# A graph layer's node stage: the second tile's relu(x - mean) on ScalarE, one step behind VectorE's moments

## The chip, the cores and the metric

The kernel runs on one core of a Trainium2 chip. The time is the device time of one execution in microseconds, as a median over several runs, and a profile is one execution with every instruction recorded. Engines are named as the profile names them: PE (TensorE, with PEld for its weight loads), DVE (VectorE), ACT (ScalarE), POOL (GpSimd) and SP (SyncE). A "q" behind a name marks what the engine's sequencer does, such as issuing a DMA.

## The reference

There are 12,500 nodes with 160 features and 400,000 edges sorted by target node. The features are normalized, passed through a relu, and sent over the edges with weights that a small network makes for each edge:

```
h = max((x - mean) / sqrt(var + 1e-5), 0)            # per node
y0, y1 = (h[:, :64] @ W_l1_0) * a, (h[:, 64:] @ W_l1_1) * a    # a: one number per node
s0, s1 = the same with W_sc0, W_sc1
w = silu(e4_len @ fc_W1 / 4) @ fc_W2 / 8             # per edge, 192 numbers
mid = products of w, y[src] and the edge's attributes # per edge
z = sum of mid over the edges of each target node
out = x + sin(pi/8) * s + cos(pi/8) * (z @ W_l2) * a
```

Because the reciprocal deviation is positive, max((x - mean) * r, 0) equals r * max(x - mean, 0). The kernel therefore computes relu(x - mean) first and applies r and a together, later, as one number per node.

## The kernel before

A tile is 128 nodes or 128 edges. There are 98 node tiles and 3125 edge tiles. The program has three parts.

**The node stage (L269 to L411)** makes y and s for all nodes. It loads x into `acc`, which stays in SBUF until the end as the sum to be written out. Its unit is a step q of two tiles (HN = 2), and four steps make a group of eight tiles (GN = 8). Ninety-eight node tiles come first, then 40 tiles of gathered rows (`xr`, fetched by gather_x() on POOL), whose y is needed by some edge blocks in edge order; that is 138 tiles in 69 steps. A step passes through these functions:

- center() on DVE: for each of the two tiles bn_stats (L326), bn_aggr (L327, mean and variance into `mv`) and h = max(x - mean, 0) (L328). In a group's last step ACT takes the square root of the variances (L332).
- scales() on DVE: in a group's last step the reciprocal (L340) and the product with a (L341), giving `ra`.
- turn_rows() on PE: four transposes into PSUM (L347, L348). out_of_psum() on ACT: their copy to SBUF as `hT` (L354).
- map_rows() on PE: the products with the weights, four matmuls a tile (L363, L364).
- leave() on ACT: the results times `ra` out of PSUM as `ys` (L375), two instructions; in a group's last step also the DMA that stores y to DRAM, issued from ACT's queue (L378 for nodes, L380 for gathered rows).
- add_s() on DVE: in a group's last step s is added to `acc` (L386), for node tiles only.

The loop at L404 writes the order out by hand: in iteration q it calls each function for step q minus a lag (scales 1, leave 4, out_of_psum 2, turn_rows 1, map_rows 3, center 0, add_s 5), in this sequence. Inside `manual_schedule` PE, ACT and DVE keep the written order; each works through its own queue and waits only where a semaphore holds it. POOL and SP are ordered by a planner, which also merges the second hand-ordered block into the first where it thinks its operands are there: so the edge weights' scaling on DVE (L234 and on) stands between two instructions of center(). In iteration 16 first_nodes() reads the edges' targets on DVE.

**relate() (L140)** follows on DVE once the node stage's last scales() is done. It turns targets into positions inside windows. The buffers that it uses are given to the main stage afterwards.

**The main stage (from L438)** goes over the edges in blocks of four tiles (GT = 4). POOL gathers y rows by an indirect DMA for each tile (L475) into `yg`, which has twelve buffers of four tiles; SP loads the edge attributes (L466, L515); PE makes the edge weights (L506), ACT scales them (L423), DVE multiplies (L429 to L436), PE sums by target (L557), and the sums of each window go through two more products into `acc` (L604).

Buffers come from pools: `nd` holds three buffers each of h and hT, `ns` three each of the small tiles (`st`, `mv`, `ra`), `nd_pt` two PSUM buffers for the transposes and `nd_po` six for the maps' results, that is three steps.

Of the kernel before, what the change touches and what calls it, by code (L numbers as in the profile page):

```python
# [10 lines left out]
F32 = mybir.dt.float32  # L11
I32 = mybir.dt.int32
AF = mybir.ActivationFunctionType
ALU = mybir.AluOpType
# [4 lines left out]
P = 128  # L19
M0 = 64  # L20
M1 = 32
D = M0 + 3 * M1
# [13 lines left out]
HN = 2  # L36
# [9 lines left out]
def kernel(  # L46
# [19 lines left out]
    nc = tc.nc  # L66
# [62 lines left out]
    def first_nodes():  # L129

        nc.vector.tensor_copy(drel, dst_i)
        nc.vector.memset(neg, -float(ZR))
        if full:
            nc.vector.tensor_reduce(neg[:, :full], drel[:, :full * WT].rearrange("p (s t) -> p s t", t=WT),
                                    AX.X, ALU.min, negate=True)
        if full < NWIN:
            nc.vector.tensor_reduce(neg[:, full:NWIN], drel[:, full * WT:T], AX.X, ALU.min, negate=True)
        nc.gpsimd.partition_all_reduce(negb, neg, P, bass_isa.ReduceOp.max)
# [61 lines left out]
    def node_weights():  # L200
        nc.vector.memset(wn0, 0.0)
        nc.vector.memset(wnr, 0.0)
        nc.scalar.dma_start(wn0[0:M0, 0, :], w_l1_0)
        nc.scalar.dma_start(wn0[0:M0, 1, :], w_sc0)
        for c in range(3):
            s = slice(M1 * c, M1 * (c + 1))
            nc.scalar.dma_start(wnr[LO + c::3, 0, s], w_l1_1)
            nc.scalar.dma_start(wnr[LO + c::3, 1, s], w_sc1)
        nc.vector.tensor_scalar(wn0[:, 0, :], wn0[:, 0, :], 1.0 / math.sqrt(M0), None, ALU.mult)
        nc.vector.tensor_scalar(wn0[:, 1, :], wn0[:, 1, :], C_S / math.sqrt(M0), None, ALU.mult)  # L210
        nc.vector.tensor_scalar(wn1[:, 0, :], wnr[:, 0, :], 1.0 / math.sqrt(M1), None, ALU.mult)
        nc.vector.tensor_scalar(wn1[:, 1, :].rearrange("p (u c) -> p c u", c=3),
                                wnr[:, 1, :].rearrange("p (c u) -> p c u", c=3), C_S / math.sqrt(M1), None, ALU.mult)

    def edge_weight_loads():
        nc.gpsimd.memset(w1, 0.0)
        for i in range(P // FC_IN):
            nc.sync.dma_start(w1[FC_IN * i:FC_IN * (i + 1), FC_H * (i % 2):FC_H * (i % 2 + 1)], fc_w1)
        for i in range(2):
            for to, of, m in ((0, 0, M0), (M0, 2 * M0, M1), (M0 + M1, M0, M0), (2 * M0 + M1, 2 * M0 + M1, M1)):  # L220
                nc.sync.dma_start(w2[FC_H * i:FC_H * (i + 1), to:to + m], fc_w2[:, of:of + m])
        nc.gpsimd.memset(wor, 0.0)

        def o1(c):
            return slice(M0 + M1 * c, M0 + M1 * (c + 1))

        nc.sync.dma_start(wor[0:M0 + M1, 0, 0:M0], w_l2_0)
        for rows, k, c in ((slice(96, P), 0, 0), (slice(0, 32), 1, 1), (slice(32, 64), 1, 2)):
            nc.sync.dma_start(wor[rows, k, o1(c)], w_l2_1[M0:, :])
        for rows, k, c in ((slice(64, P), 1, 0), (slice(0, 64), 2, 1), (slice(64, P), 2, 2)):  # L230
            nc.sync.dma_start(wor[rows, k, o1(c)], w_l2_1[0:M0, :])
# [37 lines left out]
    with (  # L269
        tc.tile_pool(name="nr", bufs=1) as nrp,  # L270
        tc.tile_pool(name="ny", bufs=2) as ny,
        tc.tile_pool(name="ns", bufs=3) as ns,
        tc.tile_pool(name="nd", bufs=3) as nd,
        tc.tile_pool(name="nd_pt", bufs=2, space=PSUM) as nd_pt,
        tc.tile_pool(name="nd_po", bufs=6, space=PSUM) as nd_po,
    ):
        yss, mvs, ras, hs, pts, hTs, poss = ({} for _ in range(7))
        loads = groups + [(NT + t, min(GN, RT - t)) for t in range(0, RT, GN)]
        steps = [(g, n, j, min(HN, n - j)) for g, n in loads for j in range(0, n, HN)]
        if RT:  # L280
# [3 lines left out]
        def load_x(g, n):  # L284
            if g + n == NT and N % P:
                nc.gpsimd.memset(acc[:, NT - 1, :], 0.0)
            node_dma(g, n, lambda rows, t, p: nc.sync.dma_start(acc[:p, g + t.start:g + t.stop, :],
                                                                by_tile(x[rows, :])))

        def gather_x():  # L290

            hi = nrp.tile([P, nr, GT], I32, name="hi")
            ai = nrp.tile([P, nr, GT], I32, name="ai")
            hf = nrp.tile([P, nr, GT], F32, name="hf")
            nf = nrp.tile([P, nr, GT], F32, name="nf")
            of = src_sb[:, RS * GT:RS * GT * (nr + 1)].rearrange("p (r c) -> p r c", c=RS * GT)[:, :, 0:GT]
            nc.vector.tensor_scalar(hi, of, 7, None, ALU.arith_shift_right)
            nc.vector.tensor_copy(hf, hi)
            nc.vector.tensor_copy(nf, of)
            nc.vector.tensor_scalar(hf, hf, -float(P * NT - 1), None, ALU.mult)  # L300
            nc.vector.scalar_tensor_tensor(nf, nf, float(NT), hf, op0=ALU.mult, op1=ALU.add)
            nc.vector.tensor_copy(ai, nf)
            table = attr.rearrange("p i -> (p i)").unsqueeze(1)
            for t in range(RT):
                c = (t // GT + 1) * RS * GT + t % GT
                nc.gpsimd.indirect_dma_start(
                    out=xr[:, t, :], out_offset=None, in_=x,
                    in_offset=bass.IndirectOffsetOnAxis(ap=src_sb[:, c:c + 1], axis=0))
                nc.gpsimd.indirect_dma_start(
                    out=ar[:, t:t + 1], out_offset=None, in_=table,  # L310
                    in_offset=bass.IndirectOffsetOnAxis(ap=ai[:, t // GT, t % GT:t % GT + 1], axis=0))

        def rows_of(g, n):
            return acc[:, g:g + n, :] if g < NT else xr[:, g - NT:g - NT + n, :]

        def center(q):

            g, n, j, m = steps[q]
            xt = rows_of(g, n)
            if j == 0:  # L320
                mvs[g] = ns.tile([P, GN, 2], F32, name="mv")
            mv = mvs[g]
            h = nd.tile([P, HN, D], F32, name="h")
            for k in range(m):
                st = ns.tile([P, 6], F32, name="st")
                nc.vector.bn_stats(st, xt[:, j + k, :])  # L326
                nc.vector.bn_aggr(mv[:, j + k, :], st)  # L327
                nc.vector.tensor_scalar(h[:, k, :], xt[:, j + k, :], mv[:, j + k, 0:1], 0.0, ALU.subtract, ALU.max)  # L328
            hs[q] = h
            if j + m == n:  # L330
                ra = ns.tile([P, GN], F32, name="ra")
                nc.scalar.activation(ra[:, :n], mv[:, :n, 1], AF.Sqrt, bias=eps)  # L332
                ras[g] = ra

        def scales(q):

            g, n, j, m = steps[q]
            if j + m == n:
                ra = ras[g]
                nc.vector.reciprocal(ra[:, :n], ra[:, :n])  # L340
                nc.vector.tensor_mul(ra[:, :n], ra[:, :n], a_sb[:, g:g + n] if g < NT else ar[:, g - NT:g - NT + n])  # L341
# [47 lines left out]
        with tc.manual_schedule(engines=engines):  # L389
            load_x(0, HN)  # L390
            nc.sync.dma_start(a_sb, attr)
            node_weights()
            load_x(HN, min(GN, NT) - HN) if NT > HN else None
            nc.sync.dma_start(src_sb, src)
            for k, (g, n) in enumerate(groups[1:]):
                load_x(g, n)
                if k == 4:
                    nc.sync.dma_start(dst_i, dst)
            if len(groups) <= 5:
                nc.sync.dma_start(dst_i, dst)  # L400
            edge_weight_loads()
            last = len(steps) - 1
            mid = len(steps) - -(-RT // HN)
            for q in range(len(steps) + 5):  # L404
                if q == min(4, last) and RT:
                    gather_x()
                if q == min(16, mid):
                    first_nodes()
                for stage, lag in ((scales, 1), (leave, 4), (out_of_psum, 2), (turn_rows, 1), (map_rows, 3), (center, 0),
                                   (add_s, 5)):  # L410
                    if 0 <= q - lag <= last:  # L411
                        stage(q - lag)
    with tc.tile_pool(name="rel", bufs=1) as rp, tc.tile_pool(name="rel_p", bufs=1, space=PSUM) as rpp:
# [24 lines left out]
    with (  # L438
# [178 lines left out]
        with order:  # L617
# [10 lines left out]
            for b in range(NB):  # L628
                g, k = divmod(b, K)
                if b + AHEAD < NB:  # L630
                    load(b + AHEAD)
                q, r = divmod(b, EG * K)
# [27 lines left out]
    with (  # L660
# [10 lines left out]
        n = nc.values_load(far_i[0:1, 0:1], min_val=0, max_val=1)  # L671
        with tc.For_i(0, n, 1) as _:
            with tc.For_i(0, ZR, P) as r:
                nc.sync.dma_start(z_d[ds(r, P), :], zero)
            with tc.For_i(0, TP // GT, 1) as g:
# [32 lines left out]
                for k in range(GT):  # L708
# [4 lines left out]
                    m = fp.tile([P, ZC], F32, name="f_m")  # L713
# [80 lines left out]
```

## Time and profile before

| | us |
|---|---|
| median of 3 runs (lowest, highest) | 4042.76 (4033.68, 4043.74) |
| the profiled execution's own time | 4041.36 |
| its span, first to last instruction | 4039.5 |
| busy in the span: PE, DVE, ACT, POOL | 3237.9, 2921.0, 2690.3, 3021.9 |
| node stage on DVE, first bn_stats to last scales() | 11.6 to 168.8 |
| relate() on DVE | 168.9 to 193.1 |
| first instruction of ACT in the main stage | 204.2 |

A row of the profile's groups reads: line, engine, operation, out<-in, shapes and count, then busy time, mean ns of one, and the idle time of the engine just before, with what ended it. A row of the timeline reads: start, duration, engine, line, operation, and in brackets the idle time before it with what released it. Two instructions in a row on one engine can overlap by some 0.1 us. The profile's times are counted from the span's start.

### The profile page before, as it was taken

The numbers are of one execution on the slowest core, as the hardware profiler recorded it, in microseconds if no ns is written. First come the engines' busy times: TensorE is split into PE (matmuls) and PEld (weight loads), VectorE is DVE, ScalarE is ACT, GpSimd is POOL, SyncE is SP. The second block draws the span as 40 slices with busy tenths as digits, with TensorE's granted clock in tenths as the row PEclk, the third lists the DMA queues.
The fourth block names the chain that finished last, engine by engine and source line by source line (L and its number), as shares of the span: only waits on it lengthen the run. The fifth ranks groups of instructions, "written<-read, shape, count | busy, mean of one in ns | idle before, by whom it ended". The sixth has DMA issues, their size and how long they took to land.

```text
span 4039.5 us, 62548 instructions
## 1 busy us (share of the span) xinstructions
PE 3237.9 (80%) x17505; PEld 2352.5 (58%) x17505; DVE 2921.0 (72%) x7558; ACT 2690.3 (67%) x9543; POOL 3021.9 (75%) x3177
## 2 busy tenths in 40 slices
PE   6689888878787887887777877887787777778887
PEld 5567666555555555555555555555555555555555
DVE  7889777777776776777776777777777767777776
ACT  5488677766666666666666666666666666666665
POOL 7667777777777777777777777777777777777776
PEclk9899999999999899999999999999999999999898
DMA  6333333222232223232223232323233222343232
GB/s 194 107 82 89 80 80 82 74 74 76 74 76 74 74 73 76 74 76 74 74 73 77 74 76 74 76 71 77 74 76 77 74 74 74 76 123 76 71 83 77
DMA packets 244949, 326.49 MB, mean 81 GB/s; under 512 B 67290, under 2 KB 194342, under 8 KB 244342
## 3 DMA queue, kind: packets, MB, share of 16 engines
q0 software_dynamic: 151280, 256.22, 25.6%
q1 hardware_dynamic: 74322, 54.52, 4.7%
q10 hardware_dynamic: 18996, 11.72, 0.9%
q8 instruction: 141, 2.31, 0.2%
q14 instruction: 210, 1.72, 0.1%
HBM read 302.92 MB, written 19.28 MB: 80 GB/s over the span
## 4 chain that ended last, share of the span: by engine, by line
DVE 23%; POOL 22%; issue 20%; DMA 20%; PE 7%; ACT 2%; DVEq 1%; ACTq 0%; POOLq 0%
POOL yg L475 22%; DMA yg<-y_d,src_sb 20%; DVE tmp L431 5%; DVE tmp L429 4%; PE pz L557 3%; DVE pr L434 3%; DVE pr L433 2%; DVE acc L604 2%; DVE sel L539 2%; DVE pr L436 2%; PE pw L506 2%; DVE pr L432 1%; DVE sel L537 1%; PE px L484 1%; ACT pw L423 1%
## 5 line engine op out<-in xcount | busy, mean ns | idle before, releaser
L475 POOL DMA_INDIRECT yg<-y_d,src_sb x3085 | 2929.8, 950 | 958.0 <-issue 749.9
L557 PE MATMUL pz<-pr,sel 128*128 128x256 f32 x6250 | 1628.1, 407 | 0.6 <-DVE pr L436 0.6
L423 ACT ACTIVATE pw<-pw,ev 128x96 f32<-128x96 f32 x3125 | 985.3, 315 | 839.9 <-PE pw L506 750.7
L557 PEld LDWEIGHTS pz<-pr,sel 128*128 128x128 f32 x6250 | 1239.5, 208 | 159.3 <-issue 0.9
L506 PE MATMUL pw<-w,hT 64*128 64x192 f32 x6250 | 761.3, 364 | 649.9 <-DVE pr L436 639.6
L506 PEld LDWEIGHTS pw<-w,hT 64*128 64x128 f32 x6250 | 516.5, 195 | 1043.1 <-DVE pr L436 874.0
L429 DVE TENSOR_TENSOR tmp<-yg,pw 128x384 f32<-128x384 f32 x782 | 432.2, 553 | 952.2 <-DMA yg<-y_d,src_sb 951.5
L564 ACT ACTIVATE zs<-pz 32x64 f32<-32x64 f32 x3126 | 669.8, 214 | 41.7
L431 DVE TENSOR_REDUCE tmp<-tmp 128x128 f32<-128x384 f32 x782 | 463.6, 593 | 27.0
L539 DVE TENSOR_TENSOR sel<-sel,pw 128x384 f32<-128x384 f32 x782 | 432.7, 553 | 26.9
L562 ACT ACTIVATE zs<-pz 32x192 f32<-32x192 f32 x1042 | 337.8, 324 | 155.4 <-PE pz L557 134.3
L434 DVE TENSOR_TENSOR pr<-pw,yg 128x384 f32<-128x384 f32 x782 | 427.0, 546 | 0.0
L484 PE MATMUL px<-xe,w 32*128 32x512 f32 x782 | 293.5, 656 | 73.2 <-issue 65.5
L489 ACT ACTIVATE hT<-px 128x512 f32<-128x512 f32 x391 | 217.7, 595 | 169.3 <-PE px L484 162.5
L432 DVE TENSOR_TENSOR pr<-pw,yg 128x256 f32<-128x256 f32 x782 | 323.4, 414 | 0.0
L433 DVE TENSOR_TENSOR pr<-pw,yg 128x256 f32<-128x256 f32 x782 | 322.6, 413 | 0.0
L537 DVE TENSOR_TENSOR sel<-iota,pw 128x128 f32<-128x128 f32 x782 | 216.5, 277 | 58.4 <-ACT pw L424 57.3
L581 PE MATMUL px<-wc,za 128*128 128x96 f32 (+1 forms) x1566 | 256.4, 304 | 0.4 <-ACT za L574 0.4
L581 PEld LDWEIGHTS px<-wc,za 128*128 128x128 f32 x1566 | 211.2, 205 | 62.7 <-issue 45.5
L595 PE MATMUL px<-os,place 128*128 128x160 f32 x1044 | 221.2, 336 | 0.5 <-ACT os L584 0.5
L436 DVE TENSOR_TENSOR pr<-pw,tmp 128x128 f32<-128x128 f32 x782 | 217.9, 279 | 0.0
L604 DVE SCALAR_TENSOR_TENSOR acc<-px,a_sb,acc 128x160 f32 x522 | 197.6, 379 | 12.6 <-PE px L595 3.3
(97 smaller groups left out, 1747.5 us busy)
## 6 DMA issues: line engine op xcount, KB each, us to landing
yg<-y_d,src_sb POOLq DMA_INDIRECT x3085
xe<-in_e SPq DMA_DIRECT2D x784, 32.0 KB
y_d<-ys ACTq DMA_DIRECT2D x12, 640.0 KB
acc<-in_x SPq DMA_DIRECT2D x11, 640.0 KB
out<-acc SPq DMA_DIRECT2D x11, 640.0 KB
raw<-in_e SPq DMA_DIRECT2D x32, 192.0 KB
yr_d<-ys ACTq DMA_DIRECT2D x5, 640.0 KB
yg<-yr_d SPq DMA_DIRECT2D x10, 320.0 KB
```

Of the source, the lines that this page charges most:

```text
L423: nc.scalar.activation(pw[:, k, 0:96], pw[:, k, 0:96], AF.Copy, scale=ev[:, k, 0:1])
L429: nc.vector.tensor_tensor(tmp[:, :n, 0:3, :], y1, wt[:, :n, NW:NW + 3].unsqueeze(3).to_broadcast([P, n, 3, M1]), ALU.mult)
L431: nc.vector.tensor_reduce(tmp[:, :n, 3, :], tmp[:, :n, 0:3, :].rearrange("p t c u -> p t u c"), AX.X, ALU.add)
L432: nc.vector.tensor_mul(pr[:, :n, 192:PC], wt[:, :n, 96:160], yg[:, :n, 0:M0])
L433: nc.vector.tensor_mul(pr[:, :n, 0:M0], wt[:, :n, 0:M0], yg[:, :n, 0:M0])
L434: nc.vector.tensor_mul(pr[:, :n, 96:192].rearrange("p t (c u) -> p t c u", c=3), wt[:, :n, M0:96].unsqueeze(2).to_broadcast([P, n, 3, M1]) ...
L475: nc.gpsimd.indirect_dma_start(out=yg[:, k, :], out_offset=None, in_=y_d, in_offset=bass.IndirectOffsetOnAxis(ap=src_sb[:, t:t + 1], axis=0))
L506: nc.tensor.matmul(pw[:, k, 0:NW], hT[r, o:o + P], w2[r, :], start=True, stop=True)
L539: nc.vector.tensor_tensor(sel[:, :, 0:3, :], sel[:, :, 3:4, :].to_broadcast([P, n, 3, WN]), wt[:, :n, NW:NW + 3].unsqueeze(3).to_broadcast ...
L557: nc.tensor.matmul(pz[:, 0:PC], sels[g][:, t % TG, :, :], pr[:, k, :], start=t % WT == 0, stop=last)
L564: nc.scalar.activation(zs[:, 192 + M0 * c:192 + M0 * (c + 1)], pz[WN * c:WN * (c + 1), 192:PC], AF.Copy)
L581: nc.tensor.matmul(po[:m, lo:hi], za[:, k, :m], wc[:, k, lo:hi], start=k == 0, stop=k == 1)
```

## The change

The second tile of each step no longer gets its h on DVE. DVE writes the negated mean into a new 128x1 tile `less` instead, and a new function, center_second(), computes relu(x + less) on ACT in the next iteration. Since h is now complete one step later, turn_rows, out_of_psum, map_rows, leave and add_s each move one step back, and the loop runs one iteration longer. The tile h moves to a pool of its own with four buffers. First tiles stay as they were.

```diff
+        tc.tile_pool(name="nh", bufs=4) as nh,
...
-            h = nd.tile([P, HN, D], F32, name="h")
+            h = nh.tile([P, HN, D], F32, name="h")
             for k in range(m):
                 st = ns.tile([P, 6], F32, name="st")
                 nc.vector.bn_stats(st, xt[:, j + k, :])
                 nc.vector.bn_aggr(mv[:, j + k, :], st)
-                nc.vector.tensor_scalar(h[:, k, :], xt[:, j + k, :], mv[:, j + k, 0:1], 0.0, ALU.subtract, ALU.max)
+                if k == 0:
+                    nc.vector.tensor_scalar(h[:, k, :], xt[:, j + k, :], mv[:, j + k, 0:1], 0.0, ALU.subtract, ALU.max)
+                else:
+                    less = ns.tile([P, 1], F32, name="less")
+                    nc.vector.tensor_scalar(less, mv[:, j + k, 0:1], -1.0, None, ALU.mult)
+                    lesses[q] = less
...
+        def center_second(q):
+
+            g, n, j, m = steps[q]
+            if m > 1:
+                nc.scalar.activation(hs[q][:, 1, :], rows_of(g, n)[:, j + 1, :], AF.Relu, bias=lesses.pop(q))
...
-            for q in range(len(steps) + 5):
+            for q in range(len(steps) + 6):
...
-                for stage, lag in ((scales, 1), (leave, 4), (out_of_psum, 2), (turn_rows, 1), (map_rows, 3), (center, 0),
-                                   (add_s, 5)):
+                for stage, lag in ((scales, 1), (center_second, 1), (leave, 5), (out_of_psum, 3), (turn_rows, 2), (map_rows, 4),
+                                   (center, 0), (add_s, 6)):
```

More of the change, by code (lines that the diff above doesn't have):

```diff
@@ L276 @@
     ):
-        yss, mvs, ras, hs, pts, hTs, poss = ({} for _ in range(7))
+        yss, mvs, ras, hs, lesses, pts, hTs, poss = ({} for _ in range(8))
         loads = groups + [(NT + t, min(GN, RT - t)) for t in range(0, RT, GN)]
```

## The prediction

> **What bounds the kernel now.** I read the list of costly groups first, then GpSimd's timeline, then walked back from it.
>
> ```profile
> L475 POOL DMA_INDIRECT yg<-y_d,src_sb x3085 | 2929.8, 950 | 958.0 <-issue 749.9
> ```
> ```profile
> 204.28 0.94 POOL L475 DMA_INDIRECT yg<-y_d,src_sb  x1 [0.30 <-issue]
> 216.88 0.95 POOL L475 DMA_INDIRECT yg<-y_d,src_sb  x1 [11.65 <-DVE pr L436]
> ...
> 4017.51 0.95 POOL L475 DMA_INDIRECT yg<-y_d,src_sb  x1 [0.30 <-issue]
> ```
>
> Of GpSimd's 958.0 us of idle time before L475, 6.56 lie before the first gather (138.49 us), 11.65 at 216.88, and the rest is a regular 0.30 per gather. 48 gathers fill the twelve yg buffers; then GpSimd waits until block 1's products free one, and from 216.88 it issues without a pause until the last, at 4018.76: 3801.9 us. The tail behind it is 4039.5 - 4018.8 = 20.7. Nothing in the change touches these two terms, 94.6% of the span. What can move is the restart at 216.88.
>
> The waits name what the restart hangs on:
>
> ```profile
> SPq L466 <- DVE far_i L183: 70.8, 1, 70.8
> ACT ev L522 <- DMA raw<-in_e: 31.5, 1, 31.5
> ```
>
> SyncE can't issue the main stage's first loads (193.21) before VectorE ends relate() (193.1); ScalarE starts at 204.22 when the last of them lands; products of blocks 0 and 1 take until 216.8. relate() starts at 168.87, right after VectorE's last scales(). So a microsecond that VectorE gains or loses in the node stage (11.6 to 168.9 us) moves the end by a microsecond. In that stage:
>
> ```profile
> 71.76:80.39 8.63, 7.13 (x49) 5.84 (x49) 7.72 (x27) 6.13 (x13) 6.80 (x7) 1.00 0.36 105
> 146.34:154.12 7.78, 7.55 (x54) 7.39 (x54) 6.41 (x27) 5.33 (x13) 5.95 (x7) 0.77 0.56 151
> 161.26:168.36 7.10, 6.31 (x48) 5.23 (x48) 6.20 (x26) 5.18 (x13) 5.44 (x6) 1.00 0.59 167
> ```
>
> Each row is one group of eight tiles, four steps (busy time of PE, weight load, DVE, ACT, POOL, then granted clock). DVE carries most (7.72 of 8.63) except in the two gathered groups at a granted clock of 0.62 and 0.77, which PE fills. A group's last step on both engines:
>
> ```profile
> 78.64 0.31 DVE L326 BATCH_NORM_STATS2 st<-acc 128x6 f32<-128x160 f32 x1
> 78.98 0.18 DVE L327 BATCH_NORM_AGGREGATE mv<-st 128x2 f32<-128x6 f32 x1
> 79.27 0.30 DVE L328 TENSOR_SCALAR h<-acc,mv 128x160 f32<-128x160 f32 x1
> 79.49 0.32 DVE L326 BATCH_NORM_STATS2 st<-acc 128x6 f32<-128x160 f32 x1
> 79.84 0.18 DVE L327 BATCH_NORM_AGGREGATE mv<-st 128x2 f32<-128x6 f32 x1
> 80.06 0.30 DVE L328 TENSOR_SCALAR h<-acc,mv 128x160 f32<-128x160 f32 x1
> 80.39 0.20 DVE L340 RECIPROCAL ra<-ra 128x8 f32<-128x8 f32 x1
> ```
> ```profile
> 78.06 1.08 ACT L375 ACTIVATE ys<-po,ra 128x320 f32<-128x320 f32 x2 [1.50 <-PE po L364]
> 79.16 0.37 ACTq L378 DMA_DIRECT2D y_d<-ys  x1
> 79.57 0.60 ACT L354 ACTIVATE hT<-pt 128x512 f32<-128x512 f32 x1 [0.44 <-ACT ys L375]
> 80.07 0.29 ACT L332 ACTIVATE ra<-mv,eps 128x8 f32<-128x8 f32 x1
> ```
>
> A DVE step has no gaps: 1.66 us, or 1.75 where an h takes 0.40. ACT reaches the square root (80.07) just as the moments are there, and DVE's reciprocal follows it at once. ACT has 1.5 us spare, in front of ys.
>
> **VectorE's removed work.** 69 second tiles lose h (L328). It took 0.30, and the next instruction began 0.22 after it did (76.67 to 76.89); in the steps of 1.75 another 0.09. In its place comes a 128x1 multiply:
>
> ```profile
> 4026.18 0.15 DVE L668 TENSOR_SCALAR spare<-lane 128x1 f32<-128x1 f32 x1
> ```
>
> 0.15 long, overlapping the next bn_stats by 0.08 as L341 does (72.00 to 72.08), so 0.07. First tiles' h starts 0.07 later after its aggregate than second tiles' (0.29 against 0.22), with an extra wait; the multiply may need that too, to reuse `less`. So an ordinary step falls from 1.65 to 1.50 or 1.57; I take 1.54, and the 0.40 form gone with h.
>
> **ScalarE's added work.** 69 Relus of 128x160 with a bias pointer. Nearest row: L375's 128x160 form, 0.39 long, two beginning 0.28 apart (169.90 to 170.45 for both); I take 0.29. The Trainium skill ("ScalarE: Activation LUTs", What ACT_TABLE_LOAD costs) gives 280 ns + 0.833 per element with a pointer bias, overlapped by 93: an estimate of 0.32 apart, 0.03 more per group on the path below. The bounds are 0.28 and 0.41 (no overlap). The same page's rules for kernel authors say that relu belongs on VectorE, not ScalarE. By that rule each moved tile costs 0.29 where it saved 0.11: a loss of 69 x 0.18 = 12 us if ACT paced the stage. The rows say it doesn't: 6.13 + 4 x 0.29 = 7.3 of 8.63. But the rule bites at one place.
>
> **The wait that it adds.** The Relu is first in ACT's queue in each iteration and can't start before VectorE's `less` of the step before. Queued behind it are two ys, hT and, in a group's last step, the square root, for which DVE's scales() wait. Counted from the start of DVE's last step: `less` visible 0.12 + Relu 0.29 + ys 0.82 (73.56 to 74.38) + hT 0.49 + square root 0.29 + release 0.03 = 2.04. DVE has its own 1.54, and so waits 0.5, where it waited 0.1 and its step was 1.75.
>
> **A group, summed.** Ordinary: scales 0.32 + 3 x 1.54 + add_s 1.40 + 2.04 = 8.38, against 8.63: -0.25. Gathered (no add_s, ys pair 0.55): the last step is 0.12 + 0.29 + 0.55 + 0.49 + 0.32 = 1.77; 0.32 + 4.62 + 1.77 = 6.71, against 7.1: -0.4.
>
> **Where it counts.** VectorE waits 2.55 us until 53.79 for the edge weights' DMA (L234); those issues on SyncE don't move, so what the first four groups gain (1.0) is given back there. Eight ordinary groups from 54 us: -2.0. Gathered groups: the two that PE fills 0, three others -1.2. Sum -3.2.
>
> **Edits at no cost.** Turns, maps, ys, the y stores on ACT's queue, and add_s come one step (1.6 to 2 us) later. The last y_d store goes at 135.1 and the first gather at 138.49; 2 us later, less what was gained, it stays hidden behind the 11.65 us that GpSimd waits before 216.88, and would cost 1:1 beyond that. The yr_d stores (172.7) are first read at 213.44. PE has 7.13 busy of a group of 8.38; no queue of SP or POOL is reordered. ys one step later no longer waits behind the reciprocal (0.52 per group on ACT), which costs nothing now and pays nothing either. `nh` with four buffers: h is read two steps later, so DVE doesn't wait for it.
>
> From the profiled execution: 4041.36 - 3.2 = 4038.2. That execution lies 1.4 below the median shown (4042.76), whose three runs spread over 10 us, or 0.25%; between the two I say **4039**.
>
> **Rivals.**
> (a) *The whole saving arrives.* If the square root isn't late (ACT running ahead of DVE), 69 steps x 0.15 to 0.23 = 10 to 16 us: 4025 to 4031, say 4029. For it: 1.5 us of ACT's slack per group. Against it: the Relu's dependency forbids ACT to run ahead.
> (b) *The square root is later than I say* (the other side). Place: ACT's queue in a group's last step. With a Relu of 0.41, the two ys waiting for PE in turn (1.08, as at 78.06), the path is 2.42, and one more PE wait like 0.5 makes it 2.9. The group is no faster than before from 2.29 on; at 2.9 it loses 0.6, over 17 groups 10 us: 4051.
> (c) *Table reloads.* If Relu isn't in the table set that holds the square root, each group pays two loads (1.28 us, the ACT_TABLE_LOAD at L332): 18 x 2.6 = 46 us, 4087. Against it: Copy alternates with the square root after a single load. The skill's same page (Table sets) says that relu is in every set; no row here shows a Relu.
> (d) *PE's clock.* It fell to 0.5 at 139.6 after PE idled; there a step took 2.5 instead of 1.8. If the new rhythm brings such stretches over eight groups, about +20: 4060. Conversely, one fewer dip gives 3 us.
>
> **How the numbers follow.** Main case 0.50 (its own range 4033 to 4046, the clock dips and the spread of the runs); (a) 0.26; (b) 0.15; (c) 0.06; (d) 0.03. 0.3%, about what a measurement of this kernel can tell from no change, is 12 us: below 4031 or above 4055. Faster: two thirds of (a) and a little of the main case, 0.20. Slower: 0.4 of (b), (c), (d), 0.15. Same 0.65. The range 4026 to 4055 leaves out the fast half of (a)'s span and the upper part of (b) with (c) and (d), together under 0.2.
>
> **What would show it.** DVE's second tile: aggregate, a 0.15 multiply, next bn_stats 0.07 later. Relu rows of 0.39 to 0.41, and three table loads in all. Before L340 a DVE wait of about 0.5 in each ordinary group, released by L332's square root, with groups of 8.4. A longer wait for edge weights near 51 us. The restart of L475 near 213.7, with 1.25 per gather behind it as before. I am wrong if the restart moves by more than 8 us, if L475 pauses after it, or if the waits before L340 are absent or above 0.8.

## The result and the profile after

The changed kernel takes 4034.15 us (median of 13 runs, 4032.54 to 4036.01); the kernel before, beside it, 4042.76 (13 runs, 4033.68 to 4043.98). The ratio is 0.9981, 95% interval 0.9972 to 0.9989: 8.6 us, or 0.2%, less. The profiled execution took 4033.11, its span 4031.3, against 4041.36 and 4039.5.

The group that carries GpSimd's gathers, from the list of costly groups of the changed kernel, and GpSimd's timeline around the restart and at the last gather:

```profile
L487 POOL DMA_INDIRECT yg<-y_d,src_sb x3085 | 2933.4, 951 | 949.0 <-issue 730.5
```
```profile
198.71 0.95 POOL L487 DMA_INDIRECT yg<-y_d,src_sb  x1 [0.31 <-issue]
205.45 0.95 POOL L487 DMA_INDIRECT yg<-y_d,src_sb  x1 [5.79 <-DVE pr L448]
...
4010.62 0.95 POOL L487 DMA_INDIRECT yg<-y_d,src_sb  x1 [0.30 <-DVE sel L551]
```

The bound is where it was: GpSimd restarts when block 1's products free a buffer, then gathers without a pause, and 20.7 us of tail follow. The restart came at 205.45 instead of 216.88, 11.43 us earlier; the last gather only 8.14 us earlier. The 3.3 us between went into the gathers themselves: 1.2533 us from one to the next over 3036 of them, against 1.2523 before. relate() starts at 158.53 instead of 168.87 and ends at 182.62 instead of 193.21.

The waits of the node stage (waiting engine, line, what released it: sum, times, longest):

```profile
ACT h L345 <- DVE less L333: 25.8, 20, 5.6
DVE ra L352 <- ACT ra L338: 5.4, 15, 0.7
DVE wc L236 <- DMA wor<-in_w_l: 1.1, 1, 1.1
```

The second row is the wait that the change adds: VectorE's reciprocal for ScalarE's square root (before, it was 1.6 us, at two places). The third is what is left of the wait for the edge weights' DMA, 2.55 us before. Three groups, by stretches of the span (busy time of PE, weight load, DVE, ACT, POOL, then granted clock):

```profile
75.75:84.09 8.34, 6.80 (x50) 5.85 (x50) 6.95 (x27) 6.97 (x18) 6.50 (x6) 1.00 0.39 110
137.37:144.23 6.86, 6.07 (x50) 5.44 (x50) 5.68 (x27) 6.13 (x18) 5.03 (x7) 1.00 0.55 155
151.21:157.99 6.78, 6.07 (x50) 5.44 (x49) 5.60 (x26) 6.13 (x18) 4.95 (x6) 1.00 0.58 158
```

An ordinary group takes 8.34 instead of 8.63; VectorE's busy time fell from 7.72 to 6.95, and ScalarE's rose from 6.13 to 6.97. The two have become equal, and neither fills the group. A group's last step, on VectorE and then on ScalarE:

```profile
73.60 0.15 DVE L333 TENSOR_SCALAR less<-mv 128x1 f32<-128x1 f32 x1
73.67 0.32 DVE L327 BATCH_NORM_STATS2 st<-acc 128x6 f32<-128x160 f32 x1
...
74.88 0.18 DVE L328 BATCH_NORM_AGGREGATE mv<-st 128x2 f32<-128x6 f32 x1
75.17 0.15 DVE L333 TENSOR_SCALAR less<-mv 128x1 f32<-128x1 f32 x1
75.75 0.20 DVE L352 RECIPROCAL ra<-ra 128x8 f32<-128x8 f32 x1 [0.43 <-ACT ra L338]
```
```profile
73.78 0.43 ACT L345 ACTIVATE h<-acc,less 128x160 f32<-128x160 f32 x1 [0.92 <-DVE less L333]
74.12 0.93 ACT L387 ACTIVATE ys<-po,ra 128x320 f32<-128x320 f32 x2
74.94 0.59 ACT L366 ACTIVATE hT<-pt 128x512 f32<-128x512 f32 x1
75.42 0.30 ACT L338 ACTIVATE ra<-mv,eps 128x8 f32<-128x8 f32 x1
```

VectorE's multiply is 0.15 long and the next bn_stats follows 0.07 after it starts. ScalarE starts the Relu when `less` of the step before is there, then does two ys and hT, and reaches the square root at 75.42, while VectorE's last aggregate was done at 75.06. So VectorE stands 0.43 before the reciprocal. ScalarE's groups show the Relu's length and its table loads:

```profile
L345 ACT ACTIVATE h<-acc,less 128x160 f32<-128x160 f32 x49 | 21.1, 431 | 24.6 <-DVE less L333 23.3 <-issue 1.4
L345 ACT ACT_TABLE_LOAD x1 | 1.3, 1283 | 6.3 <-issue 6.3
L338 ACT ACT_TABLE_LOAD x1 | 1.3, 1283 | 0.0
```

With one at L501 these are the only table loads of the execution.

### The profile page after: what moved, and what is told of

Read it like the earlier page. It is cut to its first block, busy times and chain, and to the rows that moved or that the text cites. A ratio compares the mean times of both kernels' runs of the same rounds, so it can differ in the third digit from the quotient of the medians.

```text
span 4031.3 us, 62662 instructions
## 1 busy us (share of the span) xinstructions
PE 3223.6 (80%) x17505; PEld 2346.4 (58%) x17505; DVE 2908.2 (72%) x7558; ACT 2707.0 (67%) x9612; POOL 3023.2 (75%) x3177
## 4 chain that ended last, share of the span: by engine, by line
DVE 23%; POOL 22%; DMA 21%; issue 21%; PE 5%; ACT 1%; DVEq 1%; POOLq 0%; ACTq 0%
POOL yg L487 22%; DMA yg<-y_d,src_sb 21%; DVE tmp L443 4%; DVE tmp L441 4%; DVE pr L446 3%; DVE pr L445 2%; PE pz L569 2%; DVE sel L551 2%; DVE pr L448 2%; DVE acc L616 2%; PE pw L518 1%; DVE sel L549 1%; DVE pr L444 1%; PE px L496 1%; DVE place L599 1%
## 5 line engine op out<-in xcount | busy, mean ns | idle before, releaser
L501 ACT ACTIVATE hT<-px 128x512 f32<-128x512 f32 x391 | 218.1, 595 | 167.7 <-PE px L496 160.5
```

## Experiments

### The two kernels again, side by side

The open question was where 11 us at the restart come from when the sum of the groups promised 3. Both kernels were profiled again, unchanged, in one job.

> The kernel before, unchanged, profiled on the same chip as the two beside it. Ratio 1.0. If the engines again stand still for tens of microseconds at a time, as in the runs so far (5950 us), the end says nothing and the groups of the node stage are compared in a calm stretch: 8.53 per ordinary group and 7.06 per gathered one, as the kernel before showed with only the edge weights moved; VectorE 0.1 or less before the reciprocal. If they do not: 4040, ordinary groups 8.63.

> The changed kernel, unchanged. My theory (VectorE's instructions and the root's path set a group): in a calm stretch 8.25 to 8.35 per ordinary group, 0.43 of wait before the reciprocal, so 0.2 to 0.3 below the kernel before beside it; gathered 6.8 against 7.06. The rival (most of what the first pair of traces showed was a different clock and collisions with GpSimd's issues, not the change): a calm group within 0.1 of the kernel before. Without the long stops: ratio 0.998, restart of the gathers near 205.5.

Measured: the kernel before 4035.22 (ratio to itself 0.9998, 0.9988 to 1.0007), the changed one 4027.22, ratio 0.9978 (0.9968 to 0.9987). Restart 215.54 and 205.74. Ordinary groups 8.64 and 8.34, the last three gathered ones 7.06 to 7.11 and 6.85 to 6.89, VectorE 0.43 before the reciprocal. The rival falls: the groups differ by 0.30 in both pairs of profiles. What differs beyond the groups is seen where the edge weights are scaled. VectorE's timeline, before and after:

```profile
51.35 0.18 DVE L327 BATCH_NORM_AGGREGATE mv<-st 128x2 f32<-128x6 f32 x1
53.78 0.26 DVE L234 TENSOR_SCALAR w<-w 128x192 f32<-128x192 f32 x1 [2.25 <-DMA wor<-in_w_l]
```
```profile
52.84 0.32 DVE L327 BATCH_NORM_STATS2 st<-acc 128x6 f32<-128x160 f32 x1
54.08 0.26 DVE L234 TENSOR_SCALAR w<-w 128x192 f32<-128x192 f32 x1 [0.91 <-DMA wor<-in_w_l]
```

The DMA lands at about the same time in both. But in the kernel before L234 stands behind the first aggregate of its group, at 51.5; in the changed one it stands two steps later, behind the third step's first bn_stats, with an add_s of 1.48 also ahead of it. VectorE is 2.67 us ahead there (the reciprocal at 48.02 against 50.69) and has more to do before it comes to L234: it keeps part of its lead.

### One part at a time: the later lags alone, and the Relu without them

The first edit leaves both subtractions on VectorE:

```diff
-            h = nd.tile([P, HN, D], F32, name="h")
+            h = nh.tile([P, HN, D], F32, name="h")
...
-                for stage, lag in ((scales, 1), (leave, 4), (out_of_psum, 2), (turn_rows, 1), (map_rows, 3), (center, 0),
-                                   (add_s, 5)):
+                for stage, lag in ((scales, 1), (leave, 5), (out_of_psum, 3), (turn_rows, 2), (map_rows, 4), (center, 0),
+                                   (add_s, 6)):
```

The second has all other edits of the change, so the Relu is on ScalarE, but keeps the lags of before:

```diff
-                for stage, lag in ((scales, 1), (leave, 4), (out_of_psum, 2), (turn_rows, 1), (map_rows, 3), (center, 0),
-                                   (add_s, 5)):
+                for stage, lag in ((scales, 1), (center_second, 1), (leave, 4), (out_of_psum, 2), (turn_rows, 1), (map_rows, 3),
+                                   (center, 0), (add_s, 5)):
```

> Both subtractions of a step stay on VectorE; only the later lags and the pool nh. My theory (the gain is VectorE's removed subtraction): ordinary groups 8.46 to 8.57, no wait before the reciprocal, the edge weights' wait of 2.3 us as before; 17 x 0.07 = 1.2 us, ratio 0.9995 to 1.0, restart of the gathers 1 to 2 us earlier than before. The rival (moving turns and maps back by a step is what helps, by loosening ScalarE's and TensorE's order): half the gain or more, ratio 0.999 or below, restart 5 us or more earlier.

> The Relu on ScalarE with the lags of before, so that a group's y store and ys stand in the square root's iteration. My theory: 1.0 of wait before the reciprocal and groups of 9.0 against 8.63, gathered 7.5 against 7.1: 11 x 0.35 + 5 x 0.4 = 6 us, partly paid by 1 to 2 us less wait for the edge weights; ratio 1.001 to 1.0015. The rival (VectorE's removed subtraction is worth it wherever the Relu stands): ratio 0.998 to 0.999.

Measured in one job, beside the kernel before at 4033.62: the lags alone 4030.59, ratio 0.9993 (0.9983 to 1.0002), restart at 211.05; the Relu with the old lags 4036.84, ratio 1.0006 (0.9996 to 1.0016), restart at 218.70. Neither ratio alone excludes 1.0; the restarts, against 215.54, say -4.5 and +3.2. Each restart is one profile, set against a profile of another job, and the kernel before's own two lie 1.3 apart (216.88 and 215.54); what follows rests on single rows rather than on these sums. The execution profiled in each of the two took 4038.78 and 4046.02, with gathers 1.2533 and 1.2532 us apart where the kernel before, profiled in the job above, had 1.2508; that is some 7 us over 3036 gathers, so their ends are not compared, only what lies before the restart.

For the lags alone my expectation fell: 4.5 us came, not 1 to 2. The ordinary groups are near the forecast (8.59, no wait), worth 0.3 us over six. The largest part, 2.6 us, is in the order of VectorE's queue:

```profile
54.26 1.47 DVE L387 TENSOR_TENSOR acc<-acc,ys 128x1280 f32<-128x1280 f32 x1
55.66 0.32 DVE L327 BATCH_NORM_STATS2 st<-acc 128x6 f32<-128x160 f32 x1
55.89 0.24 DVE L234 TENSOR_SCALAR w<-w 128x192 f32<-128x192 f32 x1
```

L234 stands where it stands in the changed kernel, and VectorE comes to it at 55.89, after the DMA has landed: no wait, and the two groups around it take 18.51 us instead of 21.09. With the Relu and the old lags, L234 stands behind the first aggregate again and waits:

```profile
50.61 0.18 DVE L328 BATCH_NORM_AGGREGATE mv<-st 128x2 f32<-128x6 f32 x1
52.81 0.29 DVE L234 TENSOR_SCALAR w<-w 128x192 f32<-128x192 f32 x1 [2.02 <-DMA wor<-in_w_l]
```

So it is the later lag, not the Relu, that moves L234 back. The other rival falls too: if the Relu paid wherever it stands, the ratio of the second kernel would have been 0.998 to 0.999, and its interval lies above that.

With the Relu and the old lags, ScalarE's and VectorE's timelines at the end of a group show why that group got longer than before (9.18 against 8.64):

```profile
87.01 0.43 ACT L345 ACTIVATE h<-acc,less 128x160 f32<-128x160 f32 x1
87.33 0.95 ACT L387 ACTIVATE ys<-po,ra 128x320 f32<-128x320 f32 x2
88.31 0.37 ACTq L390 DMA_DIRECT2D y_d<-ys  x1
88.72 0.60 ACT L366 ACTIVATE hT<-pt 128x512 f32<-128x512 f32 x1 [0.44 <-ACT ys L387]
89.21 0.29 ACT L338 ACTIVATE ra<-mv,eps 128x8 f32<-128x8 f32 x1
```
```profile
88.33 0.15 DVE L333 TENSOR_SCALAR less<-mv 128x1 f32<-128x1 f32 x1
89.54 0.20 DVE L352 RECIPROCAL ra<-ra 128x8 f32<-128x8 f32 x1 [1.05 <-ACT ra L338]
```

With leave four steps behind, the group's y store is issued in the same iteration as the next group's square root, and hT waits 0.44 for it; the Relu, two ys, the store and hT take 2.20 from the Relu's start to the square root, against 1.64 in the changed kernel. VectorE waits 1.05 where it waited 0.03 before, more than a group gains from four subtractions turned into short multiplies. A later lag puts the store into the iteration behind the square root.

### The Relu behind the square root

Two more kernels take away the 0.43 and the rest of the edge weights' wait. In both, center_second stands behind center in the loop, so that the square root is ahead of the Relu in ScalarE's queue, and edge_weights() is called in the node loop:

```diff
+                if q == min(30, mid):
+                    edge_weights()
-                for stage, lag in ((scales, 1), (center_second, 1), (leave, 5), (out_of_psum, 3), (turn_rows, 2), (map_rows, 4),
-                                   (center, 0), (add_s, 6)):
+                for stage, lag in ((scales, 1), (leave, 5), (out_of_psum, 3), (turn_rows, 2), (map_rows, 4),
+                                   (center, 0), (center_second, 1), (add_s, 6)):
...
-            edge_weights()
             relate(rp, rpp.tile([1, 1], F32, name="cnt"))
```

> The changed kernel with the Relu put behind the square root in ScalarE's queue, and the edge weights called in the node loop's 30th iteration. My theory: groups of 8.14 and 6.74, 0.11 before the reciprocal, no wait for the edge weights' DMA near 52 us; without the long stops 17 groups x 0.15 to 0.3 = 2.5 to 5 us below the changed kernel, so 4029 to 4032, ratio 0.997. The rival (GpSimd's gathers give an earlier restart back by a longer pitch): the restart 3 us earlier and the end where the changed kernel has it, ratio 0.998.

Measured: 4029.13, ratio 0.9984 (0.9974 to 0.9994), 2 us above the changed kernel of the same job where 2.5 to 5 us below it were expected. The waits went as expected, 0.11 before the reciprocal and none at L234, and a group took 8.24 (8.14 expected). Even so the restart came at 208.87, 3.1 us later than the changed kernel's 205.74; the pitch of the gathers was the same (1.2509 and 1.2510), so the rival falls as well. 1.25 us are there at the first reciprocal; 1.56 come in the gathered groups, at a granted clock of 0.71 and 0.72 over 18 us where the changed kernel had 0.63 over 9; and 1.5 were gained in the ordinary groups and at the edge weights. The largest piece is at the end of the stage:

```profile
162.03 1.24 DVE L143 TENSOR_REDUCE first<-negb 128x261 f32<-128x1044 f32 x1 [1.89 <-ACT h L345]
```

relate()'s first instruction now waits for the very last Relu, which in the loop's running out stands behind ys, the store and hT. The next kernel puts this one Relu first in its iteration again:

```diff
+                if q - 1 == last:
+                    center_second(last)
...
-                    if 0 <= q - lag <= last:
+                    if 0 <= q - lag <= last and (stage is not center_second or q - lag < last):
```

> The Relu behind the square root and the edge weights in iteration 30, as in root_ew, with the very last step's Relu put first in its iteration again. My theory: relate() starts right after the last scales() (0.1 instead of 1.89 us of wait), groups of 8.24 and 6.8 to 6.9 as in root_ew, so 1.8 us below root_ew beside the kernel before: ratio 0.9979, level with the changed kernel or up to 1.5 us better where TensorE's slow stretch in the gathered groups is not longer. The rival (the wait at relate() hides another that ends as late): ratio 0.9984 as root_ew.

Measured: 4025.17, ratio 0.9978 (0.9968 to 0.9987) in a job whose kernel before took 4033.62; 0.9979 was expected. The wait is 0.29, the restart 207.32:

```profile
159.13 1.24 DVE L143 TENSOR_REDUCE first<-negb 128x261 f32<-128x1044 f32 x1 [0.29 <-ACT h L345]
```

A group's end in this kernel, ScalarE's square root and Relu and VectorE's reciprocal:

```profile
73.50 0.30 ACT L338 ACTIVATE ra<-mv,eps 128x8 f32<-128x8 f32 x1 [0.84 <-DVE mv L328]
73.71 0.41 ACT L345 ACTIVATE h<-acc,less 128x160 f32<-128x160 f32 x1
```
```profile
73.58 0.15 DVE L333 TENSOR_SCALAR less<-mv 128x1 f32<-128x1 f32 x1
73.84 0.20 DVE L352 RECIPROCAL ra<-ra 128x8 f32<-128x8 f32 x1
```

ScalarE now waits for VectorE's moments, and VectorE has no more than the root's own time between aggregate and reciprocal. Even so, of the 0.43 only 0.1 per group came back (8.34 to 8.24). The end of a group is 0.32 shorter, but VectorE's own rows ahead of it are 0.24 longer: in three of a group's four steps, instead of one, the multiply starts 0.29 after its aggregate rather than 0.22, and the first subtraction takes 0.40 instead of 0.30. What delays these rows was not followed. As a version the kernel is level with the change: -8.45 us against its kernel before, where the changed kernel had -8.76 against its own. Its restart is 1.6 us later than the changed kernel's 205.74; its gathers were 1.2501 apart in that profile against 1.2510, which gives 2.6 us back by the end.

### The sum, stretch by stretch

Times are those of the reciprocals (one closes each group) on the timeline: the kernel before in us, the others as differences from it. The fifth and sixth group hold the edge weights; in the last column these are scaled in the stretch after. The 12 full groups of node tiles end at the twelfth reciprocal; the 13th closes a group of two tiles.

| stretch, by reciprocals | before | lags alone | Relu, old lags | the change | root first (last kernel) |
|---|---|---|---|---|---|
| start to 1st | 19.86 | -0.34 | -1.29 | -1.80 | -1.48 |
| 1st to 4th | 30.83 | +0.08 | +0.55 | -0.87 | -0.09 |
| 4th to 6th, edge weights | 21.09 | -2.58 | +0.15 | -2.00 | -4.62 |
| 6th to 12th, six groups | 51.83 | -0.28 | +4.10 | -1.83 | -0.70 |
| 12th to 15th, small group and two gathered | 22.12 | -1.00 | -2.14 | -1.44 | -1.32 |
| 15th to 18th, three gathered | 21.23 | +0.28 | +1.31 | -0.62 | -0.32 |
| 18th to the restart | 48.58 | -0.65 | +0.48 | -1.24 | +0.31 |
| restart | 215.54 | -4.49 | +3.16 | -9.80 | -8.22 |

The first row isn't settled: in the four profiles of kernels with the Relu and the new lags the first reciprocal lies anywhere from 18.06 to 19.31, in the three without the Relu from 19.40 to 19.86. The +4.10 of the Relu with the old lags is not all from the wait: its twelfth group took 10.05 because of one subtraction of 2.12, of the kind told in the last section, which the other kernels have in the next stretch. Against lags alone, the change gains 0.26 per ordinary group (51.55 to 50.00 over six) and 0.30 per gathered group in the last three.

### Runs in which the engines stood still

Six runs, of four kernels, belong to two earlier jobs on two other chips, where every execution, the kernel before's too, took some 5950 us. Engines stood still again and again for something that the profile doesn't show: VectorE alone was idle for over 3 us at a time in 273 to 290 places, against 18 in the kernel before of the first pair. They are told for their groups alone.

> Only the later stages (turns, maps, ys, stores, add_s one step later, h in four buffers); both tiles' h stay on VectorE. If what VectorE saves is the cause, ordinary groups stay at 8.5 to 8.63 us (at most the 0.1 us wait before the reciprocal goes), and the time is 4039 to 4043. If the later stages are the cause (ScalarE no longer held behind the reciprocal, PE fed more evenly), the groups fall to about 8.3 and the time to 4034 to 4036.

> The Relu on ScalarE with the stage lags of before, so PE's turns wait for the Relu of the same iteration. If VectorE's saving is the cause: VectorE's steps stay at 1.50 us; the square root comes a little later because ys wait for PE, a group's last step is 2.1 to 2.4 us, groups are 8.3 to 8.6, time 4034 to 4039. If the later stages are what pays: groups of 8.6 or more and 4042 or above.

> The changed kernel with the Relu moved behind the square root in ScalarE's queue. If the wait of 0.43 us before the reciprocal comes from the Relu in front of the square root: the wait falls below 0.1, ordinary groups to 7.9 to 8.0 us, gathered ones to 6.65, and the time to 4028 to 4031. If ScalarE's work as a whole paces the groups (6.97 of 8.34 busy, with the waits between), the wait only moves and the time stays at 4033 to 4035.

> The kernel before with the edge weights' scaling written into iteration 30 of the node loop, in place of where the planner puts it (it waits 2.55 us for a DMA there). If that wait is part of the 8 us that the changed kernel gained, this one gains 2 to 3 us alone: 4039.5 to 4041. If it is covered by something else (PE or ScalarE catching up meanwhile), it stays at 4042 to 4043.

> The later stages alone, again, on another chip: on the first one engines stood still for reasons outside the kernel and times near 5950 us tell nothing, but its trace has calm groups of 8.46 us. From these: ordinary groups 8.46 to 8.6 with no wait before the reciprocal. If VectorE's saving is the main cause, the time is 4038 to 4041; if the later stages are, 4034 to 4036.

> The Relu without the later stages, again. In the first chip's calm groups the wait before the reciprocal was 1.04 us (with the lags of before, the group's y store stands in ScalarE's queue in the same iteration as the square root) and a group took 9.01. If that holds here: groups near 9.0, 0.4 slower than before, over some 13 groups 5 us, the edge weights' wait perhaps gone: 4043 to 4048. If VectorE's saving alone carries the result whatever the lags: 4034 to 4038.

Here root_first is the change with center_second behind center and nothing else, before_ew the kernel before with edge_weights() in iteration 30; the others are the two kernels above. The ratios decide nothing: 0.9992 (0.9972 to 1.0012), 0.9986 (0.9968 to 1.0004), 1.0010 (0.9994 to 1.0026), 0.9987 (0.9968 to 1.0006), and in the second job 0.9980 (0.9953 to 1.0008) and 1.0013 (0.9990 to 1.0037). In stretches of the node stage without such a stop, the groups stand in the same order as later: 9.01 for the Relu with the old lags, 8.53 for the order of before (before_ew), 8.46 for the lags alone, 8.14 for the root first. They are 0.1 to 0.2 shorter than in the later runs; GpSimd had finished fetching node rows by then and issued nothing beside them, but whether that is the reason was not tested. A group of ScalarE in root_first shows the stops, as "remote":

```profile
L435 ACT ACTIVATE pw<-pw,ev 128x96 f32<-128x96 f32 x3125 | 985.3, 315 | 1646.9 <-remote 1049.1
```

What "remote" was is open.

## Why the prediction was right, and where it was not

4039 was said, 4034.15 came; the forecast of no change beyond 0.3% held, and so did the range. The sum behind it did not: -3.2 us was said for the restart, -11.4 came in the first pair and -9.8 in the second, and a move of more than 8 us was the prediction's own sign of being wrong. That the forecast held is in part luck: 0.3% of this kernel is 12 us, wide enough for more than three times the effect that was summed. In the second pair, the stretch up to the twelfth reciprocal gave 6.5 where 2.0 was said (1.8 of it ahead of the first reciprocal, which isn't settled), the small and the gathered groups 2.1 where 1.2 was said, and what lies behind the node stage 1.2 where nothing was said.

- **The bound: right.** The restart hangs on VectorE's node stage, and the gathers run on without a pause. "A microsecond moves the end by a microsecond" is nearly so: behind relate() the chain is 12.66 to 12.68 us from ScalarE's first instruction of the main stage to the restart in all eight profiles, but from relate()'s end to that instruction it took anything from 9.97 to 11.66, with no order by kernel that I can name (the last kernel has 11.23, the one before it 9.97). 1.2 us of the change's gain lies there and is unexplained.
- **VectorE's step: right.** The multiply 0.154 where 0.15 was said, 0.07 to the next instruction as said.
- **The Relu: 0.43 long, 0.32 to 0.34 to the next instruction,** where 0.39 and 0.29 were said from the row of ys. The rule of the Trainium skill that was weighed there ("ScalarE: Activation LUTs", What ACT_TABLE_LOAD costs) gave 0.32, and was the better of the two; the nearest row, of another source, was 0.03 off. The page's rule that relu belongs on VectorE doesn't hold here with the new lags: taking the Relu off VectorE brings the restart 5.3 us forward beside the lags alone (211.05 to 205.74, single profiles of two jobs; the ratios of the times are 0.9993 and 0.9978). But it bit at the place named, the square root, and with the old lags nothing is left of the gain: the restart is 3.2 us later than before, the time not clearly different (1.0006).
- **The added wait: right.** A last step of 2.08 (73.67 to 75.75) against 2.04, a wait of 0.43 against 0.5, a group of 8.34 against 8.38, gathered ones of 6.78 to 6.99 against 6.71. Of the step's terms only the Relu's was off, by 0.05. The last three gathered groups gained 0.6 in the second pair, where 1.2 was said.
- **"Where it counts": the step that failed.** "What the first four groups gain (1.0) is given back" in the edge weights' wait, which should grow. The DMA did land at about the same time, but VectorE came to L234 later in its own order, so that the wait shrank: from 2.55 to 0 there and 1.10 at L236 in the first pair, from 2.25 to 0.91 in the second. The stretch gains 2.0 us instead of giving 1.0 back. The lags alone gain 2.58 in it. I took the place of L234 for fixed; it is the planner's, and moved with the lags.
- **"Edits at no cost": the lags also pay.** Alone they bring the restart 4.5 us forward in the one profile, 2.6 of it at the edge weights; in the time itself (0.9993) this is not clear of noise. "Pays nothing either" failed; and without them the Relu gains nothing, since the y store stands ahead of the square root.
- **Left out of the sum:** the small group and the first gathered ones, where a stretch of 22 us gained 1.44. There VectorE's subtractions stretch beside GpSimd's reduction over partitions (below); in the second pair two of them were caught before, one after: 2.39 us above their usual 0.30 became 1.33. How many are caught differs by kernel (two with the lags alone), and no experiment set it.
- **The rivals.** (a) The whole saving: no, 0.43 of wait in each ordinary group; the time fell between it and the main case for another reason. (b) The late square root: not in the change, but exactly so with the old lags; a last step of 2.71 (86.83 to 89.54) made a group of 9.18, 0.54 longer, where it was said that 2.29 breaks even and 2.9 loses 0.6. (c) Table reloads: no, three loads. (d) A slower clock: no; the dip of the kernel before at 139.6 us (10.2 us at 0.5) has no counterpart in the first profile of the changed kernel, while in the second pair both have one (3.4 and 6.8 us). That may be why the restart moved by 11.4 in one pair and 9.8 in the other; it isn't settled.
- **"1.25 per gather as before"** hid a term as large as the effect: 1.2523 to 1.2533 took 3.3 us back in the first pair, and the second pair (1.2508 and 1.2510) 0.6.

## What to carry to other kernels

When work moves between two engines that follow each other in a hand-written order, look not only at the busy times but at what then stands ahead of the one instruction that the other engine waits for: here the same Relu made groups of 9.18 with a store ahead of the square root, 8.34 with the store an iteration later, and 8.24 with the square root ahead of the Relu. A lag changed for one purpose also moves the places at which a planner or a loop's end drops other work, so re-read the whole queue around every DMA wait before calling such an edit free. And where a fixed pitch is multiplied by thousands, know its spread before reading a difference of 0.2% from one profile.

## What the runs showed of the hardware

The pitch of GpSimd's indirect DMAs is not one number. The gather's group in three executions, the kernel before and the changed kernel of one job and the lags alone of the next (busy time and mean ns ahead of the idle time):

```profile
L475 POOL DMA_INDIRECT yg<-y_d,src_sb x3085 | 2926.2, 949 | 954.9 <-issue 735.8
```
```profile
L487 POOL DMA_INDIRECT yg<-y_d,src_sb x3085 | 2927.2, 949 | 948.3 <-issue 732.8
```
```profile
L476 POOL DMA_INDIRECT yg<-y_d,src_sb x3085 | 2933.5, 951 | 951.0 <-issue 745.8
```

Two nanoseconds of 950, or 7 us in 3085 gathers; over the eight profiles the distance from one gather to the next is 1.2501 to 1.2533, and two profiles of the kernel before have 1.2523 and 1.2508; the lags alone took 4038.78 in that execution and 4030.59 in the median of its ten. What sets it isn't known.

VectorE's subtraction of 128x160 stretches from 0.30 to between 0.83 and 2.12 us while GpSimd reduces over partitions. In the eight profiles eleven subtractions take longer than 0.6 us, and all eleven lie beside that reduction. In the second profile of the kernel before (GpSimd's row, then VectorE's two):

```profile
129.61 3.33 POOL L138 PARTITION_ALL_REDUCE negb<-neg  x1 [6.50 <-DVE mv L327]
```
```profile
129.55 2.08 DVE L328 TENSOR_SCALAR h<-xr,mv 128x160 f32<-128x160 f32 x1
...
132.13 0.91 DVE L328 TENSOR_SCALAR h<-xr,mv 128x160 f32<-128x160 f32 x1
```

The bn_stats between the two took 0.32 as always. A caught subtraction is not slowed by a fixed factor but held to a fixed point: six of the eleven end 2.03 us after the start of the reduction's row, whenever they began, and the other five 0.09 to 0.10 after its end. In the two kernels with the edge weights in the node loop the product L353 was caught in the same way (0.89 and 0.76 instead of 0.17). The Trainium skill ("GPSIMD Engine Reference", Specifications) says that GpSimd shares its SBUF interfaces with VectorE and contends with VectorE's instructions in a two-port mode or with two SBUF inputs; the rows agree in kind, and put a price on it, though none shows in which mode the subtraction ran. On ScalarE the same work was not caught: in the second profile of the changed kernel two Relus ran beside the reduction (125.92 and 128.77) and took their usual 0.43 each.
